# Six convolutions of v's first block between the last depthwise convolutions of q and k, on one Trainium2 core

## The chip, the cores and the metric

The kernel runs on one core of a Trainium2 chip. The metric is device time in microseconds (us) of one execution; lower is better. The engines go by the names of the profile: PE is TensorE (matrix products; PEld its weight loads), DVE is VectorE, ACT is ScalarE, POOL is GpSimd, SP is SyncE, which here only issues transfers (DMA). Each engine has its own list of instructions, and an instruction that waits for a semaphore holds what stands behind it in that list.

## The reference, cut to what matters

x has 384 channels and 192 x 192 pixels. Only layer 0 is touched by the change, and in it q, k and v up to the attention matrix:

```python
x = x + _L0_conv_ref(_gn(x), ...)
...
qkv = jnp.einsum('bchw,oc->bohw', x, w_qkv) + b_qkv[None, :, None, None]
qkv = qkv.reshape(b, 3 * c, hs, DS, ws, DS).max(axis=(3, 5))
qkv = lax.conv_general_dilated(qkv, w_dw, (1, 1), 'SAME', feature_group_count=3 * c, ...)
qkv = qkv + b_dw[None, :, None, None]
q, k, v = jnp.split(qkv, 3, axis=1)
...
attn = jnp.einsum('bhcn,bhdn->bhcd', q, k) * temperature[None]
out = _topk_softmax(attn, C // 2) @ v * a1 + _topk_softmax(attn, C * 2 // 3) @ v * a2 + ...
```

q and k are scaled to norm 1 over all pixels before `attn`, so attention needs all of q and k first. Each of q, k and v is a 1 x 1 convolution of the normalised x, a 2 x 2 maximum, and a 3 x 3 depthwise convolution. v is needed only after the top-k softmax. Layer 1, a 7 x 7 depthwise convolution of the sum, follows when all of layer 0 is done.

## The kernel before

The kernel has five stages: statistics of x (0 to about 100 us of the profiled execution), q and k (to about 1384 us), the attention matrix together with the first three blocks of v (to about 1491 us), the rest of v with the projection and the residual, and layer 1. The change lies at the border of the second and the third.

**q and k.** `for b in range(NB + 1)` (L688) runs over 24 blocks of 8 image rows. `pooled` (L592) makes, for each of the six channel groups of q and k (`ct`), three products of 512 columns in PSUM tiles `pq` (L604), and DVE takes their 2 x 2 maximum into a ring of rows (L612). One block behind, `depthwise` runs nine multiply-adds per group on DVE (`taps`, L645 and L647) into tiles `qk`, and `products` (L653) follows with the sums of squares on ACT (L656), the transposes on PE (L665), their copies to SBUF on ACT (L671), and the products of q and k, added up in the PSUM tile `grams` (L674). In the last pass, `b == NB`, there is no image block left: only the depthwise convolutions of block 23 and its `products` remain.

**Buffers.** x of q and k is loaded by SP into three buffers of `xpool`. The kernel divides PSUM into eight banks: one for `grams`, three for `ptr` (transposes and other small products), and four for `pq`. When q and k are done, `qx.close()` (L717) gives the four banks of `pq` to the pool `pv`, two tiles of two banks each, and `xctx.close()` gives the SBUF of `xpool` to what comes next: the row buffers `rows2` (filled at their borders by ACT, L508), the depthwise results `vb`, and six buffers `xp2` for x of v. A tile placed on memory that was in use before waits for the last users of that memory.

**v.** v is cut into 16 blocks (`order` sets their sequence; the first is block 13), each of six image strips `t0`, taken two at a time. `load_v` (L844) loads two strips with three transfers of 384 KB on SP (L848). `convolve` (L851) makes one of v's three channel groups for two strips: six matrix products of 384 columns (L858), which the trace shows as twelve records (1728 for 144 convolutions), and one DVE maximum of the result into rows (L864). With two `pv` tiles, a convolution can start only when the maximum of the one two before it is done.

**Attention.** `attention` (L722) is a Python generator. It takes the norms (`rn`, L725 to L728, with one step on POOL, L726), spreads them over the columns with three products against `dg_rk` (`along_free`, L218: L223 on DVE, L224 on PE, L225 on DVE), scales `grams` (L742), cuts the blocks of the heads out by small transfers (L750, issued by ACT and POOL), ranks each element against its row by fifteen DVE passes over 128 x 2304 elements (L767 to L775), makes the four softmaxes (L780 to L798), writes them into `diag` by small transfers (L804) and transposes that on PE into `attnT` (L811, L815). The loop over the first `AHEAD = 3` blocks of v draws this generator on by three steps after each pair of strips:

```python
        for i in range(AHEAD):
            for t0 in range(0, NT, UT):
                xb = load_v(i, t0)
                for ct in range(KT):
                    convolve(i, t0, ct, xb, lambda ins: ins)
                for _ in range(3):
                    next(chain, None)
```

**What sets the order.** Instructions outside a `keep` or `pin` are put in order on each engine by a scheduler at build time, by their dependencies and its own estimates of duration; so the order here is not that of the source. From block 4 of v on (`for i in range(AHEAD, NBC)`) the order on PE and DVE is written out by hand.

Of the kernel before, what the change touches and what calls it, by code (L numbers as in the profile page):

```python
# [8 lines left out]
F32 = mybir.dt.float32  # L9
AF = mybir.ActivationFunctionType  # L10
ALU = mybir.AluOpType
AX = mybir.AxisListType

P = 128
C = 384
KT = C // P
O3 = 3 * C
CT = O3 // P
HW = 192
PS = HW // 2  # L20
# [6 lines left out]
NB = PS // PR  # L27
# [24 lines left out]
TR = 32  # L52
# [17 lines left out]
RB = 2  # L70
NBC = TR // RB
PBC = NT * PS
UT = 2
FIRST = NBC - 3
# [4 lines left out]
def conv_preact_d2(  # L79
# [17 lines left out]
    nc = tc.nc  # L97
    PSUM = bass.MemoryType.PSUM
# [46 lines left out]
    wq = const.tile([P, KT, O3], F32, name="wq")  # L145
# [89 lines left out]
    def row_tiles(pool, name, n):  # L235

        t = pool.tile([P, n * KT * ROW], F32, name=name)
        rows = [
            t[:, k * ROW : (k + 1) * ROW].rearrange("p (t c) -> p t c", c=PS + 2)
            for k in range(n * KT)  # L240
        ]
        return [rows[k : k + KT] for k in range(0, n * KT, KT)], t

    vrows, rowbuf = row_tiles(rowp, "rows", 3)

    xctx = ExitStack()
    xpool = xctx.enter_context(tc.tile_pool(name="xpool", bufs=NX))
    parkp = xctx.enter_context(tc.tile_pool(name="parkp", bufs=1))

    def load_x(b, name):  # L250
        xb = xpool.tile([P, KT, BLK], F32, name=f"{name}{b}", tag="xb")
        nc.sync.dma_start(xb, xv[:, :, b * BLK : (b + 1) * BLK])
        return xb
# [5 lines left out]
    psx = ExitStack()  # L259
    pgram = psx.enter_context(tc.tile_pool(name="pgram", bufs=1, space=PSUM))  # L260
    gram = []
    for mt, (lo, hi) in enumerate(SPAN):
        o = sum(h - l for l, h in SPAN[:mt])
# [4 lines left out]
    qx = ExitStack()  # L268
# [21 lines left out]
    with tc.tile_pool(name="stp", bufs=1) as stp, tc.tile_pool(name="xsp", bufs=5) as xsp:  # L290
# [82 lines left out]
        for b in reversed(range(NB)):  # L373
            if b == NX - 1:
# [7 lines left out]
                for k, i in ((0, 0), (1, 1), (KT, 2)):  # L382
                    ps = total(f"gs_mid0_{k}", 1, terms[i])
# [6 lines left out]
            if b < NX:  # L390
                xb = held[b][:, 0:TWO]
            else:
                xb = xsp.tile([P, TWO, BLK], F32, name=f"xs{b}", tag="xs")
# [44 lines left out]
        kt = TWO  # L438
        mid = mids[:, kt : kt + 1]
        for b in [*range(NB - 2, NX, -2), NX, *reversed(range(NX))]:  # L440
            n = 2 if b > NX else 1
            if b == NX - 1:
                most = aggregate(kt, NX, NB, "most")
                ps = total(
                    "gs_mid0_2", 1,
                    [(sel(1, 2), means[1]), (shared[:, P:], me), (whole, most[:, 0:1])],
                )
# [5 lines left out]
            if b < NX:  # L453
                xb = held[b][:, kt]
            else:
                xb = xsp.tile([P, TWO, BLK], F32, name=f"xt{b}", tag="xs")
                xb = xb.rearrange("p k n -> p (k n)")[:, 0 : n * BLK]
# [3 lines left out]
        ps = total("gs0_2", 2, [(sel(1, 2), ds[1]), (shared[:, P:], de), (whole, d)])  # L461
# [23 lines left out]
    for i in range(3):  # L485
        w = wq[:, TWO, i * C : (i + 1) * C]
# [23 lines left out]
    def row_borders(tiles):  # L510
        for ct, t in enumerate(tiles):
            fill(t[:, :, 0 : PS + 2 : PS + 1], 2 * KT + ct, NT + 2, 2)
            fill(t[:, 0, :], 2 * KT + ct, PS + 2)
            fill(t[:, NT + 1, :], 2 * KT + ct, PS + 2)

    with ExitStack() as bx:
        padp = bx.enter_context(tc.tile_pool(name="padp", bufs=1))
        qkp = bx.enter_context(tc.tile_pool(name="qkp", bufs=9))
# [130 lines left out]
        def depthwise(b, ct, dst):  # L649
            r0 = b % 3 * PR  # L650
            taps(dst, ct, lambda i, j: ring[ct][:, r0 + i : r0 + i + PR, j : j + PS])

        def products(b, qk):  # L653
            for i in range(2 * KT):
                junk = trp.tile([P, PB], F32, name=f"junk{b}_{i}", tag="junk")
                nc.scalar.activation(  # L656
                    junk, qk[i].rearrange("p h w -> p (h w)"), AF.Square,
                    accum_out=ssq[:, i, b : b + 1],
                )
            for j in range(PB // P):  # L660
                sides = []
                for s in range(2):
                    ps = ptr.tile([P, C], F32, name=f"tr{b}_{j}_{s}", tag="tr")
                    for i in range(KT):
                        nc.tensor.transpose(  # L665
                            ps[:, i * P : (i + 1) * P],
                            qk[s * KT + i].rearrange("p h w -> p (h w)")[:, j * P : (j + 1) * P],
                            ident,
                        )
                    sb = trp.tile([P, C], F32, name=f"qkT{b}_{j}_{s}", tag=f"qkT{s}")  # L670
                    nc.scalar.copy(sb, ps)  # L671
                    sides.append(sb)
                for mt, (lo, hi) in enumerate(SPAN):
                    nc.tensor.matmul(  # L674
                        gram[mt],
                        sides[0][:, mt * P : (mt + 1) * P],
                        sides[1][:, lo:hi],
                        start=False,
                        stop=(b == NB - 1 and j == PB // P - 1),
                        skip_group_check=True,  # L680
                    )


        nc.tensor.matmul(
# [3 lines left out]
        for b in range(NB + 1):  # L688
            xb = None
            if b < NB:  # L690
                xb = held.pop(b) if b in held else load_x(b, "xq")
            qk = []
            for ct in range(2 * KT + 1):
                if b < NB and ct < 2 * KT:
                    if b == 0 and ct < 2:

                        if ct == 0:
                            pooled(b, 0, xb)
                            pooled(b, 1, xb)
                            biases()  # L700
                    else:
                        pooled(b, ct, xb)
                    bordered(b, ct)
                if b > 0 and ct > 0:
                    dst = qkp.tile([P, PR, PS], F32, name=f"qk{b}_{ct}", tag="qk")
                    qk.append(dst)
                    depthwise(b - 1, ct - 1, dst)
                    if ct == 2 * KT:
                        products(b - 1, qk)
            if b == 2:  # L710
                for tiles in vrows:
                    row_borders(tiles)
            if b < len(pieces):
                with tc.issue_after(stats0):
                    weights(*pieces[b])

    qx.close()  # L717
    xctx.close()

    near = {}  # L720
# [100 lines left out]
    rowp2 = dx.enter_context(tc.tile_pool(name="rowp2", bufs=1))  # L821
    vp = dx.enter_context(tc.tile_pool(name="vp", bufs=6))
    xp2 = dx.enter_context(tc.tile_pool(name="xp2", bufs=6))
    pv = psx.enter_context(tc.tile_pool(name="pv", bufs=2, space=PSUM))
    H = PBC // 2
    order = [(FIRST + i) % NBC for i in range(NBC)]

    vrows += row_tiles(rowp2, "rows2", 2)[0]
    for tiles in vrows[3:]:
        row_borders(tiles)  # L830

    def place(i):

        i %= NBC
        return vrows[i] if i < 2 else vrows[2 + (i - 2) % 3]

    def image_rows(ct, b, t0, nt):
        return bass.AP(
            x.tensor,
            x.offset + (ct * P * HW + t0 * TR + b * RB) * HW,  # L840
            [[HW * HW, P], [TR * HW, nt], [1, RB * HW]],
        )

    def load_v(i, t0):  # L844
        b = order[i]
        xb = xp2.tile([P, KT, UT, RB * HW], F32, name=f"xv{b}_{t0}", tag="xv")
        for kt in range(KT):
            nc.sync.dma_start(xb[:, kt], image_rows(kt, b, t0, UT))  # L848
        return xb

    def convolve(i, t0, ct, xb, pin):  # L851
        b, rows = order[i], place(i)
        o = (2 * KT + ct) * P
        ps = pv.tile([P, UT, 512], F32, name=f"pv{b}_{t0}_{ct}", tag="pv")
        for u in range(UT):
            for kt in range(KT):
                pin(
                    nc.tensor.matmul(  # L858
                        ps[:, u, 0 : RB * HW], wq[:, kt, o : o + P], xb[:, kt, u, :],
                        start=(kt == 0), stop=(kt == KT - 1),  # L860
                    )
                )
        pin(
            nc.vector.tensor_reduce(  # L864
                rows[ct][:, 1 + t0 : 1 + t0 + UT, 1 : PS + 1],
                ps[:, :, 0 : RB * HW].rearrange("p u (a w b) -> p u w a b", a=2, b=2),
                AX.XY,
                ALU.max,
            )
        )  # L870


    vbs, begun = {}, set()
# [29 lines left out]
    with tc.tile_pool(name="ap", bufs=1) as ap:  # L903
        chain = attention(ap)
        for i in range(AHEAD):
            for t0 in range(0, NT, UT):
                xb = load_v(i, t0)
                for ct in range(KT):
                    convolve(i, t0, ct, xb, lambda ins: ins)
                for _ in range(3):  # L910
                    next(chain, None)
            if i == AHEAD - 1:
                for ct in range(KT):
                    depthwise_v(1, ct, (0, 1))
        for _ in chain:
            pass
# [148 lines left out]
    for i in range(AHEAD, NBC):  # L1065
        j = i - 2
        xb = load_v(i, 0)
# [4 lines left out]
        xb = load_v(i, UT)  # L1072
# [9 lines left out]
        xb = load_v(i, 2 * UT)  # L1082
# [40 lines left out]
    with ExitStack() as ex_:  # L1123
# [97 lines left out]
        with tc.tile_pool(name="gps1", bufs=1, space=PSUM) as gps:  # L1221
            ps = over_groups(gps, mid1.unsqueeze(2), 1, "gs_mid1")
            gmid = const.tile([P, KT], F32, name="gmid")
            nc.vector.tensor_scalar_mul(gmid, ps[:, :, 0], 1.0 / GC)
            ps = over_groups(gps, about(mv1, gmid, "1"), 2, "gs1")
# [133 lines left out]
        last = None  # L1359
        for n in range(steps):  # L1360
# [9 lines left out]
            for q in range(CP):  # L1370
                ps = pc.tile([P, 2, 512], F32, name=f"pc{n}_{q}", tag="pc")
                for k in range(2):
                    i = 2 * q + k
# [9 lines left out]
                            start=False, stop=False,  # L1383
# [5 lines left out]
                            start=False, stop=True,  # L1389
# [20 lines left out]
            last = apart  # L1410
# [57 lines left out]
```

## Time and profile before

| what | value |
|---|---|
| median of 4 runs | 2834.36 us (2829.42 to 2846.21) |
| the profiled execution | 2846.21 us, its span 2844.5 us |
| granted PE clock over the span | 0.982 |
| PE busy | 2649.5 us, 93% of the span |
| DVE busy | 2319.8 us, 82% |
| ACT busy, POOL busy | 871.1 us (31%), 760.3 us (27%) |
| PE busy from 1240 to 1300 us (q and k, steady) | 59.95 of 60.00 us |
| PE busy from 1384.05 to 1399.17 us | 14.14 of 15.12 us |
| PE busy from 1399.17 to 1490.77 us | 91.60 of 91.60 us |
| DVE busy from 1399.17 to 1490.77 us | 78.62 of 91.60 us |
| PE busy from 1490.77 to 2844.5 us | 1287.82 of 1353.73 us |

The profiled execution is the slowest of the four runs, 11.85 us over their median; sums below are made within it. The span is the time from the first to the last instruction; 1.7 us of the execution lie outside it. Times of single instructions are counted in us from the start of the span. Busy shares are averages over stages with different limits: at the border of q, k and v PE is the busy engine on both sides, and a stretch of some 25 us between them is not full. A PE that is busy is not always at full speed: the column PEclk gives the clock that was granted, 1.00 being full.

### The profile page before, as it was taken

To read this page: it belongs to the slowest core of one execution; us is meant where nothing else is said; L and a number is where in the kernel's file an instruction comes from. 1 tells how busy PE (TensorE), PEld (TensorE's weight loads), DVE (VectorE), ACT (ScalarE), POOL (GpSimd) and SP (SyncE) were. 2 spreads that over 40 slices of the span, in tenths; PEclk is the share of its full clock that TensorE was granted. 3 is DMA by queue.
4 is the path that set the end of the run, shared out by engine and by line. 5 is a ranking of instruction groups with operands and counts; after the bars stand their busy time and mean duration, and the time that the engine had idled before them with its cause. 6 is when DMAs were issued, how large, how long until landed. Compare 5 with 4: busy or idle time off the path is not lost.

```text
span 2844.5 us, 25466 instructions
## 1 busy us (share of the span) xinstructions
PE 2649.5 (93%) x8671; PEld 1585.0 (56%) x8671; DVE 2319.8 (82%) x3382; ACT 871.1 (31%) x1637; POOL 760.3 (27%) x884
## 2 busy tenths in 40 slices
PE   0399999999999999999899989999998699999997
PEld 0244444444444454444556656666666477777776
DVE  7989887878878788788688878888889678777776
ACT  0141111111111111111102322222324467777775
POOL 1034444000000000000102330010101467788887
PEclk9999999999999999999999999999999799999999
DMA  9966766201011010100336998575666899999997
GB/s 382 401 237 223 250 202 232 100 34 67 34 53 47 34 67 33 39 28 0 134 103 211 335 363 270 176 250 187 227 222 216 295 313 356 372 366 372 366 371 249
DMA packets 236401, 584.52 MB, mean 205 GB/s; under 512 B 16704, under 2 KB 168112, under 8 KB 219504
## 3 DMA queue, kind: packets, MB, share of 16 engines
q1 hardware_dynamic: 175344, 286.77, 29.2%
q0 software_dynamic: 37376, 148.85, 15.4%
q10 hardware_dynamic: 23552, 147.27, 13.8%
q8 instruction: 69, 1.13, 0.2%
q14 instruction: 60, 0.49, 0.0%
HBM read 374.47 MB, written 208.21 MB: 205 GB/s over the span
## 4 chain that ended last, share of the span: by engine, by line
PE 79%; DMA 12%; DVE 5%; POOL 2%; ACT 1%; issue 1%; SPq 0%; ACTq 0%; POOLq 0%; DVEq 0%
PE pq L604 37%; PE pv L858 19%; DMA out_dram<-res 6%; PE pr L970 4%; PE pc L1387 3%; PE pc L1376 3%; PE pc L1381 3%; PE po L946 3%; DMA xs<-in_x_dram 2%; PE grams L674 2%; PE tr L665 2%; PE pq_begun L423 1%; DVE st L318 1%; DVE vb L892 1%; DMA xv<-in_x_dram 1%; DMA sd<-sx 1%
## 5 line engine op out<-in xcount | busy, mean ns | idle before, releaser
L604 PE MATMUL pq<-xq,wq 128*128 128x512 f32 x2268 | 990.7, 592 | 0.0
L604 PEld LDWEIGHTS pq<-xq,wq 128*128 128x128 f32 x2268 | 423.0, 190 | 492.2 <-issue 447.0
L647 DVE SCALAR_TENSOR_TENSOR qk<-ring,wd,qk 128x384 f32<-128x384 f32 x1152 | 674.1, 612 | 20.9 <-ACT ring L634 7.1
L858 PE MATMUL pv<-xv,wq 128*128 128x384 f32 x1728 | 567.4, 489 | 10.2 <-DMA xv<-in_x_dram 9.2
L858 PEld LDWEIGHTS pv<-xv,wq 128*128 128x128 f32 x1728 | 329.5, 191 | 237.1 <-DMA xv<-in_x_dram 8.0
L612 DVE TENSOR_REDUCE ring<-pq 128x128 f32<-128x512 f32 x428 | 293.7, 687 | 190.7 <-PE pq L604 189.9
L1400 DVE TENSOR_SCALAR apart<-pc,rb 32x576 f32<-32x576 f32 x384 | 312.3, 813 | 128.8 <-PE pc L1387 111.5
L1398 ACT ACTIVATE apart<-pc,rb 32x576 f32<-32x576 f32 x384 | 281.4, 733 | 146.5 <-PE pc L1387 141.7
L892 DVE SCALAR_TENSOR_TENSOR vb<-rows,wd,vb 128x576 f32<-128x576 f32 x384 | 313.0, 817 | 11.2
L1387 PE MATMUL pc<-aux,h 128*128 128x288 f32 x768 | 251.0, 408 | 4.2 <-POOL aux L1309 2.7
L1376 PE MATMUL pc<-main,w 128*128 128x288 f32 x768 | 251.7, 409 | 0.3 <-issue 0.3
L1381 PE MATMUL pc<-main,w 128*128 128x288 f32 x768 | 250.9, 408 | 0.0
L1004 DVE TENSOR_TENSOR sx<-xr,y 128x576 f32<-128x576 f32 x192 | 217.5, 1174 | 39.1 <-ACT y L978 23.4
L656 ACT ACTIVATE junk<-qk 128x384 f32<-128x384 f32 x144 | 75.4, 523 | 541.7 <-DVE qk L647 541.7
L1346 POOL COPY res<-apart 128x1152 f32<-128x1152 f32 x96 | 212.7, 2247 | 90.6 <-DMA out_dram<-res 63.8
L755 POOL MEMSET lower<- 128x2304 f32 x1 | 2.0, 2018 | 871.7 <-PE grams L674 871.7
L1045 POOL DMA_DIRECT2D sd<-sx x96 | 72.2, 756 | 511.3 <-DVE sx L1004 491.8
L864 DVE TENSOR_REDUCE rows<-pv 128x192 f32<-128x768 f32 x144 | 137.5, 956 | 67.8 <-PE pv L858 67.6
L1387 PEld LDWEIGHTS pc<-aux,h 128*128 128x128 f32 x768 | 145.6, 190 | 48.6 <-POOL aux L1324 4.2
L1381 PEld LDWEIGHTS pc<-main,w 128*128 128x128 f32 x768 | 146.6, 191 | 42.0
L1376 PEld LDWEIGHTS pc<-main,w 128*128 128x128 f32 x768 | 146.2, 191 | 42.4 <-issue 1.0
L1024 ACT ACTIVATE wq<-sx,negmid 128x1152 f32<-128x1152 f32 x96 | 120.6, 1257 | 101.3 <-DVE sx L1004 97.2
(214 smaller groups left out, 2348.3 us busy)
## 6 DMA issues: line engine op xcount, KB each, us to landing
sd<-sx POOLq DMA_DIRECT2D x96, 600.0 KB, 10.3
xv<-in_x_dram SPq DMA_DIRECT2D x144, 384.0 KB, 5.1
xr<-in_x_dram SPq DMA_DIRECT2D x48, 1152.0 KB, 15.1
out_dram<-res SPq DMA_DIRECT2D x192, 288.0 KB, 10.8
main<-sd ACTq DMA_DIRECT2D x46, 1200.0 KB, 9.9
xq<-in_x_dram SPq DMA_DIRECT2D x21, 2304.0 KB, 8.8
w<-wt ACTq DMA_DIRECT2D x46, 1024.0 KB, 7.0
xs<-in_x_dram SPq DMA_DIRECT2D x24, 1536.0 KB, 15.1
```

The lines of the kernel that those rows point to most:

```text
L604: nc.tensor.matmul(ps, wq[:, kt, ct * P : (ct + 1) * P], rows[:, kt, :, g * 64 : (g + 1) * 64], start=(kt == 0), stop=(kt == KT - 1), skip ...
L612: nc.vector.tensor_reduce(t[:, r0 : r0 + PR, 1 + g * 32 : 1 + (g + 1) * 32], ps.rearrange("p (h a w b) -> p h w a b", h=PR, a=2, b=2), AX. ...
L647: nc.vector.scalar_tensor_tensor(dst, src, w, dst, ALU.mult, ALU.add)
L858: nc.tensor.matmul(ps[:, u, 0 : RB * HW], wq[:, kt, o : o + P], xb[:, kt, u, :], start=(kt == 0), stop=(kt == KT - 1),)
L892: pin(nc.vector.scalar_tensor_tensor(dst, src, w, dst, ALU.mult, ALU.add))
L1004: nc.vector.tensor_tensor(bass.AP(flat.tensor, flat.offset + at(e) + a * RUN, [flat.ap[0], [JP, NT], [1, NJ], [at(f) - at(e), 2]],), xq[:, ...
L1346: keep(nc.gpsimd.tensor_copy(res[:, k], apart[:, :, k].rearrange("p e n -> p n e")))
L1376: nc.tensor.matmul(acc, w[:, i, 0:P], main[:, i, :, 0:NJ], start=True, stop=False)
L1381: nc.tensor.matmul(acc, w[:, i, P : 2 * P], main[:, i, :, 1 : 1 + NJ], start=False, stop=False,)
L1387: nc.tensor.matmul(acc, h[:, i], aux[:, i, :, 0:NJ], start=False, stop=True,)
L1398: keep(nc.scalar.mul(dst, src, scale))
L1400: keep(nc.vector.tensor_scalar_mul(dst, src, scale))
```

## The change

The three helpers `order`, `place` and `image_rows`, and `convolve`, are moved up unchanged, ahead of the stage on q and k. In the last pass of that stage (`b == NB`) the banks of `pq` are now released at its start and `pv` opened there; x of the first four strips of v's first block is loaded into a buffer of `xpool` (three transfers of 768 KB on SP); and after every second depthwise convolution (`ct` 2, 4 and 6) two of the six convolutions on these strips are put into the program. `products` returns its last matrix product, and in the loop over the first three blocks of v the remaining 21 convolutions are to be issued only after it. The third pair of strips of the first block still uses `load_v`. Nothing is computed that was not computed before, and nothing is left out.

```diff
             xb = None
             if b < NB:
                 xb = held.pop(b) if b in held else load_x(b, "xq")
+            else:
+
+                qx.close()
+                pv = psx.enter_context(tc.tile_pool(name="pv", bufs=2, space=PSUM))
+                xb = xpool.tile([P, KT, 2 * UT, RB * HW], F32, name="xv_begun", tag="xb")
+                for kt in range(KT):
+                    nc.sync.dma_start(xb[:, kt], image_rows(kt, order[0], 0, 2 * UT))
             qk = []
...
                     depthwise(b - 1, ct - 1, dst)
+                    if b == NB and ct % 2 == 0:
+                        for n in range(ct - 2, ct):
+                            t0 = n // KT * UT
+                            convolve(0, t0, n % KT, xb[:, :, t0 : t0 + UT], lambda ins: ins)
                     if ct == 2 * KT:
-                        products(b - 1, qk)
+                        multiplied = products(b - 1, qk)
...
-    qx.close()
     xctx.close()
...
         for i in range(AHEAD):
             for t0 in range(0, NT, UT):
-                xb = load_v(i, t0)
-                for ct in range(KT):
-                    convolve(i, t0, ct, xb, lambda ins: ins)
+                if i > 0 or t0 == 2 * UT:
+                    xb = load_v(i, t0)
+                    with tc.issue_after(multiplied):
+                        for ct in range(KT):
+                            convolve(i, t0, ct, xb, lambda ins: ins)
                 for _ in range(3):
                     next(chain, None)
```

In `products` the loop's last statement keeps the instruction for the caller:

```diff
-                    nc.tensor.matmul(
+                    last = nc.tensor.matmul(
...
-                    )
+                    ).ins
+            return last
```

## The prediction

> **What bounds the kernel now.** The chain of waits first: PE holds 79% of it.
>
> ```profile
> PE 79%; DMA 12%; DVE 5%; POOL 2%; ACT 1%; issue 1%; SPq 0%; ACTq 0%; POOLq 0%; DVEq 0%
> ```
>
> The chain by time shows where PE is not its holder near the change: DVE (`qk` L647) from 1359.58 to 1376.91 us, then POOL and DVE (`lower`, `rn`, `dg_rk`) from 1384.1 to 1392.1. The timeline of PE there (start, duration, instructions, in brackets the idle time before and its releaser):
>
> ```profile
> 1359.38 1.56 PE L665 MATMUL tr<-ident,qk 128*128 128x128 f32 x10
> ...
> 1370.37 1.33 PE L665 MATMUL tr<-ident,qk 128*128 128x128 f32 x5 [2.74 <-DVE qk L647]
> ...
> 1376.93 0.69 PE L665 MATMUL tr<-ident,qk 128*128 128x128 f32 x2 [3.55 <-DVE qk L647]
> 1378.00 3.57 PE L674 MATMUL grams<-qkT,qkT 128*128 128x144 f32 x12 [0.38 <-ACT qkT L671]
> ```
>
> PE waits for the last depthwise convolutions, and works slowly in between: the same twelve products took 1.79 us at 1312.80. The table of windows has the clock (columns: PE, PEld, DVE, ACT, POOL busy, PEclk, DMA share, GB/s):
>
> ```profile
> 1367.00:1369.00 2.00, 0.63 (x5) 0.42 (x3) 2.00 (x5) 1.87 (x8) 0.00 (x0) 1.00 0.00 0
> 1369.00:1371.00 2.00, 0.63 (x3) 0.63 (x4) 2.00 (x5) 0.62 (x2) 0.00 (x0) 0.55 0.00 0
> 1371.00:1373.00 2.00, 1.64 (x9) 1.23 (x7) 1.93 (x5) 0.99 (x3) 0.00 (x0) 0.50 0.00 0
> ...
> 1383.00:1385.00 2.00, 2.00 (x11) 1.55 (x11) 0.30 (x1) 0.00 (x0) 0.84 (x1) 1.00 1.04 375
> ```
>
> From 1399 us PE is full again; the timeline of DVE shows what runs beside it, and that the attention matrix is early:
>
> ```profile
> 1399.01 91.75 PE L858 MATMUL pv<-xv,wq 128*128 128x384 f32 x284
> 1490.60 0.93 PE L811 MATMUL aT<-ident,diag 128*128 128x128 f32 x7
> ```
> ```profile
> 1384.24 0.30 DVE L725 TENSOR_REDUCE rn<-ssq 128x6 f32<-128x144 f32 x1 [7.36 <-PE grams L674]
> ...
> 1388.81 2.40 DVE L223 TENSOR_SCALAR dg_rk<-ident,rn 128x128 f32<-128x128 f32 x2
> ...
> 1472.54 0.30 DVE L798 TENSOR_TENSOR mix<-mix,em 128x144 f32<-128x144 f32 x1
> 1475.32 0.96 DVE L864 TENSOR_REDUCE rows<-pv 128x192 f32<-128x768 f32 x1 [2.49 <-PE pv L858]
> ```
>
> `mix` is done at 1472.84; its transfers are issued until 1476 and land 1.6 to 1.8 us later, some 13 us before PE comes to `aT`.
>
> **What the skill says.** The Trainium skill, "TensorE: Matmul & The Clock Gate", Part 1, says that an idle window of about 3.4 us halves PE's clock and about 3.4 us of work restore it. The trace agrees roughly: 1.00 before 1369, 0.50 from 1371, back some 5 us after work resumed at 1378.0. "SBUF — State Buffer", section "Who interferes with whom", says that DVE's fast two-port forms and POOL exclude each other for a whole instruction; here one of the three `dg_rk` took 2.209 us against a median of 0.285, and ended with POOL's `affine_select` (1388.48 to 1390.93).
>
> **The most that can be had.** From 1359.38 to `aT` at 1490.60 are 131.2 us. PE's own work in them: 27 convolutions of twelve records at 0.3226 us (284 records in 91.6 us), 3.87 us each, 104.5 us; two blocks' `tr` and `grams` at 4.7 us (8.12 us from 1308.34 to 1316.46, less eight `pq` records, 3.4 us), 9.4; `tps` and `af_rk`, 1.7. Sum 115.6. Idle time and half clock are thus 15.6 us, 0.55% of the execution: the ceiling. On every engine the lists before this stretch and from block 4 of v on hold the same instructions in the same order in both programs (only SP has three transfers fewer, in the stretch), so a gain at `aT` shifts what follows by as much.
>
> **Part by part.** I lay durations of the trace along the changed program's lists.
>
> *The six convolutions*: 72 records, 23.2 us of PE, all ahead of block 23's transposes. The load of 3 x 768 KB waits only for block 21's products (done by about 1257 us) while DMA is idle: hidden. The banks of `pq` are free when DVE's last maximum ends (1360.28): no wait. Block 22's transposes and products are interleaved with the first convolution and end at about 1368.0 (8.6 us of PE from 1359.4); the other five follow without a stop, to 1387.4. DVE has 16.5 us of `qk` and four maxima of 0.95 us inside it; each falls due in time (about 1368.7, 1373.8, 1377.9, 1380.8), because DVE's 0.53 to 0.63 us per multiply-add leaves a gap for every 3.87 us of PE.
>
> *Products later*: in the new list all transposes of block 23 stand behind the sixth convolution; they need `qk`, ready at 1380. From 1387.4: transposes, ACT's copies (0.42 us each, with two and then seven border fills of 0.26 us ahead of or among them; these fills now wait for the sixth convolution, since `rows2` lies on its x), products; PE idles about 1 us in bits. Last product at about 1393.1, against 1384.05: 9.0 us later.
>
> *The load of the third pair*: it and all of v's loads behind it on SP now wait for the sixth convolution, 1387.4 instead of 1377.0, for memory. A load lands 3.4 to 8.4 us after issue, median 4.7: about 1392.2, just before PE can use it at 1393.1. I take 0; at worst about 2 us. Later loads are needed 3.87 x 3 us apart and are not late.
>
> *The norms*: the chain from the last product to `dg_rk` is the old one, with `lower` (2.02 us, POOL) ahead of `rn` again: 7 us, to 1400.1. In the old list PE had 17 products of v ahead of it (34 records); in the new one only five (ten records, 3.2 us), then `af_rk` waits. PE stands from 1396.3 to 1400.1: 3.8 us. Half clock afterwards: the 2.74 us gap at 1367.6 was followed by it, so I count it, 2.3 us for PE; below 0 it cannot cost.
>
> So at about 1402.6 PE has done 84 records where the old run had done about 51: a lead of 33 records, 10.7 us.
>
> *The attention chain on DVE* starts 9 us late with fewer convolutions left beside it (19 maxima instead of 23 at its first pass). The new DVE list puts three passes of 2.55 us (`rank`, `eq`, `gt` of the second and third third) between two maxima, and later two maxima side by side. Laid out: `gt` begins at 1408.8; maxima at 1413.7, 1417.2, 1420.6, 1424.1, 1430.1, 1433.5, 1437.0; then the three passes to 1445.4, while PE has finished block 14's eighth convolution at 1442.7 and needs the seventh's tile, free at 1446.35: PE waits 3.6 us. After that DVE stays a little ahead; `mix` ends at 1477.1, its transfers at 1481.8, PE's last convolution at 1485.1. At full clock after the norms the same sum gives 1483.9. So `aT` starts at about 1484.6, 6.0 us early.
>
> Sum within the profiled execution: 15.6 ceiling, less stops that replace the old: 1.0 (copies), 3.8 (`af_rk`), 0 to 2.3 (clock, partly swallowed by the next), 3.6 (PSUM tile behind DVE), about 1 for waits on semaphores: 5 to 7. 2846.21 - 6 = 2840.2. The median of the shown runs is 11.85 us lower; I take the gain as the same: 2834.36 - 6 = 2828.4.
>
> **Rivals.** (1) *PE stays the bound after the norms*: the load is on time, and DVE's order doesn't stall PE. For it: DVE was busy only 78.62 of 91.60 us in that stretch. Against: the order of the list is fixed, and three passes in a row leave PE without a tile. It gives the lead of 10.7 to 11.5 us: 2823. (2) *Slower: the attention chain becomes the path.* Place: from the last product to `aT`. In the old run the chain takes 1384.05 to 1477.5, 93.5 us, and has 13 us to spare; it now starts 9.0 us late, so from 97.5 us on the kernel is slower. By my sum it shortens to 88.7, mostly as four maxima of 0.95 us are gone from it; if late loads (the burst of 27 filled DMA from 1379 to 1399 in the old run), the small `att` transfers behind that burst, and PE at half clock hold DVE's maxima, which stand between its passes, it grows. Price: 3 us above break-even at 100 us: 2837. (3) *Returned later*: a fixed transfer rate in the rest of v takes the gain back, 0: 2834. For: DMA share 0.84 after 1490.77. Against: those transfers are issued by the same shifted lists.
>
> **Chances.** Forecast 0.62, rival 1 0.16, rival 2 0.14, rival 3 0.08. A measurement of this kernel tells about 0.5%, 14 us, from no change. The ceiling of 15.6 us hardly passes that, rival 2 would need a chain of 112 us; with the spread of the runs (2829 to 2846) faster by over 0.5% gets 0.11, slower 0.05, same 0.84. The range holds the cases and the spread of a median: 2819 to 2839.
>
> **What would show it.** PE: six convolutions between 1360 and 1388 with no gap over 1 us; the last `grams` near 1393; a gap of about 4 us before `af_rk`; a gap of 3 to 4 us released by DVE `rows` near 1443; `aT` near 1484.6; and the same distance from `aT` to the end. It is wrong if `aT` lies outside 1479 to 1490, or if that distance changes.

## The result, and the profile after

| | before | after |
|---|---|---|
| median | 2834.99 us (64 runs) | 2830.55 us (43 runs) |
| ratio to before | | 0.9983, 95% interval 0.9974 to 0.9991 |
| profiled execution, its span | 2846.21, 2844.5 us | 2836.47, 2834.8 us |

The changed kernel takes 4.4 us less; the interval makes it 2.6 to 7.4 us. Predicted were 6.0. A second set of runs agrees: 22 of the changed kernel with a median of 2831.61 us against 33 of before with 2837.43 us, ratio 0.9981 (0.9969 to 0.9992).

The spans differ by 9.7 us, and not all of it is the change. I measure from here on D, the distance from the first `tr` behind the last `pq` to the first `aT` on PE: in before from 1359.38 to 1490.60, 131.2 us. In after PE's timeline has (start, duration, line and engine, operation, records, in brackets the idle time ahead and its releaser):

```profile
1355.54 1.50 PE L700 MATMUL tr<-ident,qk 128*128 128x128 f32 x10
...
1364.32 19.51 PE L537 MATMUL pv<-xv_begun,wq 128*128 128x384 f32 x60
1383.67 1.67 PE L700 MATMUL tr<-ident,qk 128*128 128x128 f32 x12
...
1389.33 3.39 PE L537 MATMUL pv<-xv,wq 128*128 128x384 f32 x10
1396.61 1.20 PE L224 MATMUL af_rk<-dg_rk,ones 128*128 128x128 f32 x4 [3.89 <-DVE dg_rk L223]
...
1441.68 38.97 PE L537 MATMUL pv<-xv,wq 128*128 128x384 f32 x120 [3.05 <-DVE rows L543]
1480.49 0.93 PE L857 MATMUL aT<-ident,diag 128*128 128x128 f32 x7
```

D is 124.95 us, 6.3 less. The stage begins 3.8 us earlier in this execution, which came from the stages ahead of it, where both programs hold the same instructions in the same order but for the three early transfers. PE's clock from 190 to 200 us was 0.83 in before and 1.00 in after; it was 0.83 in both_orders too (an experiment below), whose program is after's up to this stretch and which begins it at 1358.69. So I take the 3.8 us as spread between executions; no run isolates them. From `aT` to the end it is 1353.9 us before and 1354.3 after. So 3.8 + 6.3 - 0.4 is the difference of the spans. D is what the change moved.

The table of windows shows the two halves of D and the rest (columns: PE, PEld, DVE, ACT, POOL busy, PEclk, DMA share, GB/s):

```profile
1355.54:1389.43 33.89, 33.87 (x152) 23.14 (x151) 22.41 (x37) 12.10 (x40) 0.00 (x0) 1.00 0.12 41
1389.43:1480.49 91.06, 84.08 (x260) 49.13 (x259) 80.32 (x92) 1.51 (x6) 11.87 (x14) 0.98 0.43 142
1480.49:2834.80 1354.31, 1287.96 (x4786) 910.29 (x4784) 1100.39 (x1268) 652.54 (x1009) 584.87 (x596) 0.97 0.84 290
```

To the last product PE is full and at full clock: the three stops for DVE `qk` are gone. Of the next 91 us it stands 7.0, in two stops: 3.89 us for `dg_rk` and 3.05 us for a maximum. What holds the second is in the timeline of DVE: three ranking passes in a row, then two maxima that PE has been waiting for.

```profile
1433.29 2.54 DVE L821 TENSOR_REDUCE rank<-gt 128x48 f32<-128x2304 f32 x1
1435.75 2.54 DVE L815 TENSOR_TENSOR eq<-att 128x2304 f32<-128x2304 f32 x1
1438.21 2.54 DVE L813 TENSOR_TENSOR gt<-att 128x2304 f32<-128x2304 f32 x1
1440.68 1.81 DVE L543 TENSOR_REDUCE rows<-pv 128x192 f32<-128x768 f32 x2
```

The chain of waits over the whole span has changed little, as most of the span is the other stages:

```profile
PE 79%; DMA 11%; DVE 6%; ACT 1%; POOL 1%; issue 1%; ACTq 0%; SPq 0%; POOLq 0%; DVEq 0%
```

### The profile page after: what moved, and what is told of

It reads as the page before. It is cut to its first block, busy times and chain, and to the rows that moved or that the text cites. A ratio compares the mean times of both kernels' runs of the same rounds, so it can differ in the third digit from the quotient of the medians.

```text
span 2834.8 us, 25467 instructions
## 1 busy us (share of the span) xinstructions
PE 2644.3 (93%) x8671; PEld 1581.1 (56%) x8671; DVE 2314.4 (82%) x3382; ACT 871.1 (31%) x1637; POOL 762.8 (27%) x884
## 4 chain that ended last, share of the span: by engine, by line
PE 79%; DMA 11%; DVE 6%; ACT 1%; POOL 1%; issue 1%; ACTq 0%; SPq 0%; POOLq 0%; DVEq 0%
PE pq L639 37%; PE pv L537 18%; DMA out_dram<-res 6%; PE pr L983 4%; PE pc L1400 4%; PE pc L1389 3%; PE pc L1394 3%; PE po L959 3%; DMA xs<-in_x_dram 2%; PE grams L709 2%; PE tr L700 2%; PE pq_begun L423 1%; DVE st L318 1%; DVE vb L903 1%; DMA aux<-sh 1%; DMA sd<-sx 1%
## 5 line engine op out<-in xcount | busy, mean ns | idle before, releaser
L537 PE MATMUL pv<-xv,wq 128*128 128x384 f32 x1656 | 545.4, 490 | 11.4 <-DVE rows L543 6.6
L537 PEld LDWEIGHTS pv<-xv,wq 128*128 128x128 f32 x1656 | 316.2, 192 | 229.8 <-DVE rows L543 8.9
## 6 DMA issues: line engine op xcount, KB each, us to landing
sd<-sx POOLq DMA_DIRECT2D x96, 600.0 KB, 10.5
```

Of the source, the lines that this page charges most:

```text
L537: nc.tensor.matmul(ps[:, u, 0 : RB * HW], wq[:, kt, o : o + P], xb[:, kt, u, :], start=(kt == 0), stop=(kt == KT - 1),)
```

## The experiments

All of them are read by D, because single executions of one kernel spread over more than 20 us (after: 2822.41 to 2844.28).

| kernel | D, us | PE's stops over 0.6 us behind the last `grams` |
|---|---|---|
| before, before_again | 131.2, 131.4 | `rows`, about 1.0 each (the stops for `qk` lie ahead of the last `grams`) |
| after, after_again, after_third | 125.0, 127.6, 127.4 | `dg_rk` 3.89 each; `rows` 3.05, 2.74, 2.74 |
| six_behind | 139.2 | `dg_rk` 0.80, `xv` 1.74, `rows` 3.76 |
| three_ahead | 129.2 | `dg_rk` 0.80, `xv` 1.81, `rows` 0.94 |
| af_late | 128.6 | `dg_rk` 0.70, `rows` 1.38, 5.52, 0.92 |
| chain_late | 134.7 | `dg_rk` 3.60, `rows` 2.74, `diag` 7.04 |
| dve_order | 121.7 | `dg_rk` 2.49, `rows` 0.79 |
| both_orders | 119.1 | none |
| orders_mended | 117.2 | `rows` 0.83 |

**Is it the filled gaps? six_behind.** The load, its buffer and the early banks stay; the convolutions go behind the products.

```diff
-                    if b == NB and ct % 2 == 0:
-                        for n in range(ct - 2, ct):
-                            t0 = n // KT * UT
-                            convolve(0, t0, n % KT, xb[:, :, t0 : t0 + UT], lambda ins: ins)
                     if ct == 2 * KT:
                         multiplied = products(b - 1, qk)
+                    if b == NB and ct == 2 * KT:
+                        with tc.issue_after(multiplied):
+                            for n in range(2 * KT):
+                                t0 = n // KT * UT
+                                convolve(0, t0, n % KT, xb[:, :, t0 : t0 + UT], lambda ins: ins)
```

> D (first `tr` after the last `pq` to the first `aT` on PE) is 131.2 us before, 125.0 us after. Here the early load, the buffer and the early banks stay as in after, and the six convolutions are issued only behind the last product of q and k. Theory (the gain is PE's filled gaps alone; the load from the buffer and the banks bring nothing): the stops for DVE `qk` and the half clock are back, about 25 us to the last `grams` as in before; moreover the load of the third pair waits for the sixth convolution, so PE stops some 4 us there: D is 133 to 137, worse than before. Rival (the early load and the early banks carry the gain): D stays near 125.

D was 139.2. PE's timeline:

```profile
1366.42 1.33 PE L700 MATMUL tr<-ident,qk 128*128 128x128 f32 x5 [2.85 <-DVE qk L682]
...
1372.97 0.69 PE L700 MATMUL tr<-ident,qk 128*128 128x128 f32 x2 [3.48 <-DVE qk L682]
1374.05 3.57 PE L709 MATMUL grams<-qkT,qkT 128*128 128x144 f32 x12 [0.38 <-ACT qkT L706]
...
1407.57 7.98 PE L537 MATMUL pv<-xv,wq 128*128 128x384 f32 x24 [1.74 <-DMA xv<-in_x_dram]
1419.30 75.49 PE L537 MATMUL pv<-xv,wq 128*128 128x384 f32 x228 [3.76 <-DVE rows L543]
```

The old stops for `qk` are back, and the twelve products take 3.57 us again; the last product ends after 24.8 us, in before after 24.7. So the early load and banks carry nothing by themselves; the rival is out. The load of the third pair is issued at 1404.17, behind the sixth convolution, and PE waits for it, 1.74 us where I had expected some 4: the buffer has a price, which after pays under the products of block 23. The 3.76 us for a maximum I had not expected; DVE's timeline has the reason:

```profile
1413.35 2.56 DVE L814 TENSOR_TENSOR gt<-att 128x2304 f32<-128x2304 f32 x1 [5.93 <-DMA att<-scaled]
1415.83 2.55 DVE L816 TENSOR_TENSOR eq<-att 128x2304 f32<-128x2304 f32 x1
1418.30 0.95 DVE L543 TENSOR_REDUCE rows<-pv 128x192 f32<-128x768 f32 x1
```

The small transfers into `att` now run at the same time as the late loads. They land 5.1 us after issue in the median, in after 2.8, and DVE waits 5.93 us for them, with two passes and then PE's maximum behind them in its list. (In after the wait is 0.59 us, but there other work fills part of the 3.1 us between `scaled` and `gt`.) It is the place that the prediction's second rival named, in a kernel where the loads come late. With the half clock behind it (0.96 and 0.61 in the two windows of 4 us from 1416), it puts D 2 us above the theory's range.

**How many? three_ahead.** After every second depthwise convolution one convolution instead of two, the other three behind the products.

```diff
-                        for n in range(ct - 2, ct):
-                            t0 = n // KT * UT
-                            convolve(0, t0, n % KT, xb[:, :, t0 : t0 + UT], lambda ins: ins)
+                        n = ct // 2 - 1
+                        convolve(0, 0, n, xb[:, :, 0:UT], lambda ins: ins)
...
+                            for n in range(KT):
+                                convolve(0, UT, n, xb[:, :, UT : 2 * UT], lambda ins: ins)
```

> D is 131.2 us before, 125.0 us after. Here three of the six convolutions stay ahead of block 23's products and three stand behind them. Theory (every convolution placed in the gaps is worth its 3.87 us until about 10.6 us of gaps are full, but the load of the third pair, which waits for the sixth, is now late by about 4 us): last `grams` 26 to 28 us after the start (before 24.7, after 33.9), a stop of about 4 us for the load before the first convolution of the third pair, no stop of 3.9 us before `af_rk`, D 126 to 129. Rival (three would do, because the norms and the ranking then start 6 us earlier): D 124 or less.

The last product ended at 27.7 us, as expected. Then:

```profile
1394.83 0.61 PE L224 MATMUL af_rk<-dg_rk,ones 128*128 128x128 f32 x4
1396.24 0.49 PE L224 MATMUL af_rk<-dg_rk,ones 128*128 128x128 f32 x2 [0.80 <-DVE dg_rk L223]
1398.54 10.95 PE L537 MATMUL pv<-xv,wq 128*128 128x384 f32 x24 [1.81 <-DMA xv<-in_x_dram]
1410.43 73.80 PE L537 MATMUL pv<-xv,wq 128*128 128x384 f32 x228 [0.94 <-DVE rows L543]
```

Between the end of the sixth convolution (1395.0) and the first on the third pair PE has 3.5 us with only 1.1 us of work, and 24 records behind it take 10.95 us instead of 7.9: half clock. The stop for the load is 1.81 us, not the 4 expected. D was 129.2, 0.2 above the range. The clock was low twice, the first time behind stops of at most 1.45 us:

```profile
1376.00:1380.00 4.00, 3.86 (x19) 3.51 (x19) 0.00 (x0) 1.43 (x4) 0.00 (x0) 0.66 0.00 0
1380.00:1384.00 4.00, 4.00 (x13) 3.38 (x13) 0.30 (x1) 0.00 (x0) 1.29 (x1) 0.50 0.00 0
```

Each time costs up to some 3.4 us of PE's work (4 x (0.34 + 0.50) here, and 4 x (0.28 + 0.50 + 0.07) in the three windows from 1396 to 1408), 6.8 in all; after lost 1.7 to 5.1 us in this way, as the part on the firmness of D works out. So this one execution does not show that three ahead are worse than six: the clock alone can make the difference of 1.6 to 4.2 us. The rival, D of 124 or less, did not come true. Three ahead with the third pair loaded earlier was not tried.

**Which of after's two stops costs? af_late.** The matrix products of the norms stand behind 18 products of v instead of 5; DVE's order is left to the scheduler.

```diff
-        along_free(rkb, rn[:, KT : 2 * KT], ptr, "rk", "tr")
+        with tc.issue_after(done[0]):
+            along_free(rkb, rn[:, KT : 2 * KT], ptr, "rk", "tr")
...
-                for _ in range(3):
+                for _ in range(3 if i > 0 else 9 if t0 == 2 * UT else 0):
                     next(chain, None)
```

(`done[0]` is the last product of v traced by then.)

> D is the distance from the first `tr` after the last `pq` to the first `aT` on PE: 131.2 us before, 125.0 us after. Here `af_rk` stands behind 18 products of v (36 records) instead of 5 (10 records); the order on DVE follows by itself and now has four ranking passes in a row (`rank`, `eq`, `gt`, `eq`) between two maxima, and three of them once more. Theory (what the change leaves is two stops of PE, and the second is set by the order on DVE): the stop of 3.9 us before `af_rk` and the half clock behind it go, but PE then stops for DVE `rows` about 5 to 6 us and once more 3 to 4 us, so D is 126 to 128: no gain. Rival (the stop before `af_rk` is the whole loss and DVE keeps up): D falls by about 4 to 5 us, to 120 to 121.

The stop of 3.89 us is gone and D is 128.6, no better than after:

```profile
1415.83 11.88 PE L539 MATMUL pv<-xv,wq 128*128 128x384 f32 x36 [1.38 <-DVE rows L546]
1433.23 10.67 PE L539 MATMUL pv<-xv,wq 128*128 128x384 f32 x24 [5.52 <-DVE rows L546]
1444.82 38.97 PE L539 MATMUL pv<-xv,wq 128*128 128x384 f32 x120 [0.92 <-DVE rows L546]
```

All of it comes back as stops for DVE, which now has four passes between two maxima, as its timeline shows:

```profile
1422.36 2.54 DVE L825 TENSOR_REDUCE rank<-gt 128x48 f32<-128x2304 f32 x1
1424.82 2.55 DVE L819 TENSOR_TENSOR eq<-att 128x2304 f32<-128x2304 f32 x1
1427.28 2.55 DVE L817 TENSOR_TENSOR gt<-att 128x2304 f32<-128x2304 f32 x1
1429.75 2.55 DVE L821 TENSOR_TENSOR eq<-eq,lower 128x2304 f32<-128x2304 f32 x1
1432.22 0.95 DVE L546 TENSOR_REDUCE rows<-pv 128x192 f32<-128x768 f32 x1
```

The rival (the stop before `af_rk` is the whole loss and DVE keeps up) is out. As DVE's order changed along with PE's, this run does not weigh the two stops against each other; the next two do.

**DVE's order: dve_order, both_orders.** The 21 convolutions, their maxima and the steps of `attention` are traced in a written order, held by `keep` on PE and DVE. One word stands for one convolution, traced first; then `M` is the maximum of the oldest open one, `c` the next step of `attention` (with one ranking pass each), `t` a multiply-add of `vb`.

```diff
+        plan = 'ccc Mcctt Mtcc Mc Mc Mc Mc Mcc Mc Mc Mc Mc Mcc Mc Mccc Mcc Mc M Mttttt Mttttt MtttttM'.split()
+        late = []
+        for n, acts in enumerate(plan):
...
+                convolve(i, t0, ct, xb, keep, late)
+            for act in acts:
+                if act == "M":
+                    late.pop(0)()
...
+                elif act == "c":
+                    next(chain)
```

In both_orders the same is done with the norms further back, so that `af_rk` stands behind three convolutions, and with three tiles `dg_rk` instead of two. In both, `tps` has moved behind the last products, and a stop of 0.68 us for ACT opens ahead of these.

```diff
-        plan = 'ccc Mcctt Mtcc Mc Mc Mc Mc Mcc Mc Mc Mc Mc Mcc Mc Mccc Mcc Mc M Mttttt Mttttt MtttttM'.split()
+        plan = 'c Mc Mc Mcctt Mtcc Mc Mc Mc Mc Mcc Mc Mc Mc Mc Mcc Mc Mccc Mcc Mcttttt Mttttt MtttttM'.split()
```

> D is 131.2 us before and 125.0 us after. Here PE's order is that of after but for one product ahead of `af_rk`, and DVE's order is written out: one ranking pass, twice two, between two maxima of v. Theory: the stop before `af_rk` stays (3 to 4 us, with its short half clock), the stop of 3.05 us for DVE `rows` goes and no other takes its place, so D is 120 to 122. Rival (DVE's total work in the stretch, not its order, holds PE): the stop only moves to a later maximum and D stays at 124 to 125.

> D is 131.2 us before and 125.0 us after; PE's own work in it is about 115.6. Here `af_rk` stands behind three whole convolutions and DVE's order is written out as in dve_order. Theory (the two stops are all that the change leaves): no stop of PE over 0.6 us between the last `grams` and `aT`, the clock stays at 1.00, `mix` is done about 9 us before PE comes to `aT`, D is 117 to 118.5, and the time some 13 us under before and 7 us under after, as the distance from `aT` to the end (1354 us) stays. Rival (the attention chain becomes the path once PE has no stops): PE stops before `aT`, D 120 to 125. Rival (what is gained at `aT` is given back later): D 117 to 118.5 but the distance from `aT` to the end grows to 1360.

dve_order: D 121.7. The stop before `af_rk` is 2.49 us; that for DVE has shrunk to 0.79, and up to `aT` no other over 0.3 takes its place. The clock stayed at 1.00, where I had expected a short half clock, so a part of the distance to after (125.0 to 127.6) is the clock:

```profile
1395.83 0.68 PE L793 MATMUL af_rk<-dg_rk,ones 128*128 128x128 f32 x4 [2.49 <-DVE dg_rk L792]
...
1409.56 46.71 PE L538 MATMUL pv<-xv,wq 128*128 128x384 f32 x144 [0.79 <-DVE rows L544]
```

both_orders: D 119.1, 0.6 above the range, with no stop over 0.6 us behind the last `grams` and the clock at 1.00 throughout; its median was 2826.96 us against 2837.43 of before, ratio 0.9964 (0.9949 to 0.998). Both stops are thus mainly DVE's and PE's order: DVE does the same ranking passes and softmaxes in all of them. Its work up to `aT` is not quite the same, 102.7 us in after, 100.1 in dve_order and 96.4 in both_orders, as some multiply-adds of `vb` now stand behind `aT`. There PE stops for DVE `rows`, for 0.87 us in dve_order and for 1.56 and 0.87 us in both_orders, and not at all in after; so a part of the gain in D is paid back there.

**The small rest: orders_mended.** both_orders still stops four times for 0.23 to 0.51 us, and twice behind `aT`. Here nine of the eighteen `t`, instead of three, stand ahead of the first ranking pass, where DVE waits for the norms and for `att`; their own order is changed too. The doubled passes are spread, and `tps` stands ahead of the last product, as in after.

```diff
-        plan = 'c Mc Mc Mcctt Mtcc Mc Mc Mc Mc Mcc Mc Mc Mc Mc Mcc Mc Mccc Mcc Mcttttt Mttttt MtttttM'.split()
+        plan = 'c Mtttc Mtttc Mccttt Mc Mc Mcc Mc Mc Mc Mc Mcc Mc Mc Mc Mcc Mcc Mcc Mccttt Mttt MtttM'.split()
```

> D is 131.2 us before, 125.0 and 127.6 us in two runs of after, 119.1 us in both_orders, where PE still stops four times for DVE `rows` for 0.2 to 0.5 us (each with about 0.27 us for the first product behind it), 0.7 us before the last products, and twice more (1.6 and 0.9 us) just behind `aT`. Here nine multiply-adds of `vb` are moved from the end of the stretch into DVE's early idle time, the two ranking passes in a row are spread evenly, and `tps` stands ahead of the last products again. Theory (these small stops come from DVE being late by what was packed into its last slots): D 117 to 118, the stop behind `aT` at most 0.9 us, the time 1 to 4 us under both_orders, about 13 us under before. Rival (DVE is simply full here): D stays at 119.

```profile
1386.81 11.77 PE L538 MATMUL pv<-xv,wq 128*128 128x384 f32 x36
1398.42 0.83 PE L795 MATMUL af_rk<-dg_rk,ones 128*128 128x128 f32 x6
1399.09 66.33 PE L538 MATMUL pv<-xv,wq 128*128 128x384 f32 x204
1466.25 4.14 PE L538 MATMUL pv<-xv,wq 128*128 128x384 f32 x12 [0.83 <-DVE rows L544]
1470.22 0.93 PE L871 MATMUL aT<-ident,diag 128*128 128x128 f32 x7
```

One stop is left, and D is 117.2, 1.6 above PE's own work of 115.6. No stop follows behind `aT`, and DVE's work up to there is 100.3 us. The median of 9 runs is 2821.66 us, against 2835.12 of before in 14 runs: 0.9951 (0.9932 to 0.9969). By this ratio the version beats both kernels (after had 0.9983, 0.9974 to 0.9991); the two were not measured side by side.

**How far is the attention chain from the path? chain_late.**

```diff
+        for _ in range(14):
+            nc.scalar.copy(ex, mix)
+            nc.scalar.copy(mix, ex)
         diag = ap.tile([P, KT, C], F32, name="diag")
```

> D is 131.2 us before, 125.0 us after. Here 28 copies of `mix` on ACT, about 8 us in a row, are put between the last `mix` and the transfers into `diag`; nothing else moves and no result changes. It asks how far the attention chain is from the path. Theory (in after the chain's last transfer lands some 3.7 us before `aT`): PE stops before `aT` for the added time less 3.7 us, about 4 us, D about 129. Rival (the chain is as far from the path as in before, 13 us): no stop, D 125. Rival (it is already on it): D 133.

The copies took 0.34 us each, from 1473.71 to 1483.35, so 9.6 us instead of 8. PE's and ACT's timelines:

```profile
1489.57 1.95 PE L860 MATMUL aT<-ident,diag 128*128 128x128 f32 x7 [7.04 <-DMA diag<-mix]
```
```profile
1483.35 3.30 ACTq L853 DMA_DIRECT2D diag<-mix  x5
```

9.6 us of delay make a stop of 7.0, so the chain had 2.6 us to spare, in place of the 3.7 I had expected. The other two theories, 13 us to spare and none, are out. The 2.6 us are a low figure, because the delayed transfers fell into other transfers (DMA share 0.98 and 1.06 from 1484 to 1488) and took longer to land. From issue to landing they took 4.8 to 5.5 us here, 2.6 to 3.5 in after and 1.6 to 1.8 in before. As an estimate from this, in after itself the last of them, issued at 1474.3, has landed by 1477.8, which leaves 2.7 us or somewhat more before `aT` at 1480.49. In before the last is issued at 1475.4, which leaves the 13 us of the prediction.

**How firm is D? after_again, before_again, after_third.** No edit.

> The changed kernel once more, for the spread of D from run to run. Theory: D within 0.7 us of 124.95, the distance from `aT` to the end within 2 us of 1354.3, while the start of the stretch moves by some us with the statistics stage; the total ratio to before is near 0.998. Rival (the 6.3 us at `aT` were themselves such a spread): D differs by 3 us or more.

> The kernel before once more, for the spread of D, which was 125.0 and 127.6 us in two runs of after: PE's clock falls to half behind some of its stops of 2.7 to 3.9 us and not behind others. Theory: before has only one such place (the stops for DVE `qk`, where PE waits for DVE in any case), so D is within 1 us of 131.2 and PE's clock is 1.00 from the last `grams` to `aT`. Rival (D of before spreads as that of after): 129 or less, or 133 or more.

> The changed kernel a third time. Theory: D is between 124.5 and 128, and what it has above 124.5 stands as half clock behind the stop before `af_rk` and behind the stop for DVE `rows`: half clock behind both gives about 127.5, behind the first alone about 125. Rival (the spread has another source): D outside of this, or not accounted for by the clock within 0.7 us.

before gave 131.4, within 0.2 of the first, and its clock was 1.00 from the last `grams` to `aT` as expected. after gave 127.6 and 127.4, neither within 0.7 of the first nor 3 off: here my theory for after_again failed. The table of windows shows why. First after, then after_again:

```profile
1396.00:1400.00 4.00, 3.40 (x10) 2.59 (x11) 1.81 (x5) 0.00 (x0) 0.38 (x1) 0.57 0.92 312
1400.00:1404.00 4.00, 4.00 (x14) 2.37 (x13) 3.96 (x9) 0.00 (x0) 2.40 (x5) 1.00 0.37 112
...
1444.00:1448.00 4.00, 4.00 (x14) 2.36 (x13) 4.00 (x4) 0.00 (x0) 0.00 (x0) 1.00 0.28 46
```
```profile
1396.00:1400.00 4.00, 3.16 (x9) 2.46 (x10) 1.81 (x4) 0.00 (x0) 0.61 (x1) 0.51 0.94 315
1400.00:1404.00 4.00, 4.00 (x9) 2.21 (x8) 3.68 (x8) 0.00 (x0) 2.17 (x5) 0.63 0.42 129
...
1444.00:1448.00 4.00, 4.00 (x9) 2.22 (x8) 4.00 (x3) 0.00 (x0) 0.00 (x0) 0.59 0.00 0
```

In after the clock is low in one of these windows, which loses 4 x 0.43 = 1.7 us; in after_again in three, which loses 4 x (0.49 + 0.37 + 0.41) = 5.1 us. The difference of 3.4, less 0.3 by which the second stop is shorter, is 3.1; D differs by 2.6. after_third has half clock behind both stops too (0.50 and 0.79, then 0.83 and 0.75), and D of 127.4, as expected for that case. The median gain of 4.4 us lies between the three values of 131.3 - D (131.3 is the mean of the two of before): 6.3, 3.8 and 3.9.

**Is the gain given back behind `aT`?** From `aT` to the end the profiled executions range from 1335 to 1354 us, those of one kernel too (before 1353.9 and 1340.9), so single runs can't tell. In six_behind, three_ahead and chain_late, run together, D is 139.2, 129.2 and 134.7, and the rest is 1336.5, 1336.2 and 1335.2: there it doesn't follow D. In before_again, after_third and orders_mended, also run together, it is 1340.9, 1351.4 and 1353.4, longer where D is shorter. The medians decide: orders_mended gains 14.1 us in D and 13.5 in the median (8.8 to 19.3 by the interval), both_orders 12.2 and 10.5 (5.7 to 14.5). So the gain is not given back as a whole; that a few us of it are, these intervals can't exclude.

## Why the prediction was right, and where its sizes were off

The forecast, the likeliest case, held by place and by sign. By its steps, times from the stage's start in before (1359.38) and after (1355.54):

- *Six convolutions without a stop*, their end predicted at 28.0 us: 28.1. PE was busy 33.87 of 33.89 us to the last products.
- *Last product 9.0 us later*, at 33.7: 33.9.
- *The third pair's load costs 0*: no stop there. That it was a cover and not a gift is shown by six_behind and three_ahead, where PE waits for it.
- *PE stands 3.8 us before `af_rk`*: 3.89, three times.
- *PE waits 3.6 us for a PSUM tile behind DVE's passes*: 3.05, 2.74, 2.74.
- *Half clock after the norms, 2.3 us*: the mis-sized term. It was 1.7 us in the first run and 3.4 in after_again; and behind the second stop the prediction counted none, where after_again has 1.6. The forecast of 6.0 was thus good for the profiled execution (6.3), which had the best clock of the three, and that much is luck; it was too high for the other two (3.8, 3.9), and against the median it is 1.6 us too much.
- *The closing sum*: 15.6 less 1.0, 3.8, 3.6, about 1 and 0 to 2.3 is 3.9 to 6.2, not the "5 to 7" that stands there; the 6.0 comes from the times laid out before it. In after what is lost of the 15.6 is 9.3: 3.89 and 3.05 for the stops, 1.7 for the clock, nothing for ACT's copies, and some 0.7 for the rest.
- *`aT` at 125.2 us*: 125.0, 127.6, 127.4.
- *Rival 1 (PE stays the bound after the norms)* failed for the reason given: DVE's fixed order. dve_order shows that the stop goes with the order. *Rival 2 (the chain becomes the path)* did not happen, and was near: the sum left 3.3 us between the last transfer and PE, chain_late shows 2.6. *Rival 3 (the gain is returned later)* fell with the medians above, as far as it says all of the gain.

Of the ceiling of 15.6 us the change takes 4 to 6, because two stops and their half clock replace the old ones; orders_mended takes 14.1.

## What to carry to other kernels

A gap on the busy engine that is filled with later work moves everything that hung on the order of that later work: look what else used to stand between the same waits (here the cover of the norms and the maxima between ranking passes), and give it a new cover in the same edit. Where two engines hand tiles to and fro with two buffers, look at the longest run of other work between two releases and not only at the sum of work: one 2.5 us pass between two maxima of 0.9 us held PE's 3.87 us step, three did not. When the difference is a fifth of a per cent, measure a distance inside the profile, over several executions, and compare the clock granted in it.

## What the runs showed of the hardware that I had not expected

Whether half clock follows a stop of PE of about 3 us differs from one execution to the next. The stop of 3.89 us was followed by it each time, which cost 1.7 us of PE's work in after and 3.4 in after_again; one of 2.74 us was followed by it in after_again, after_third and chain_late; one of 3.05 us in after was not, nor was one of 2.49 us in dve_order. The Trainium skill, "TensorE: Matmul & The Clock Gate", Part 1, says that the window by which activity is judged runs freely, so that the place of the change depends on where work falls in it; the runs agree in that the same program has it in one execution and not in another. They don't agree with its 3.4 us as the least idle time: 2.74 us sufficed, and in three_ahead the clock fell behind three stops of 0.16, 1.45 and 0.64 us with transposes between them (PE busy 1.87 of 4.00 us from 1372 to 1376).

DVE's `dg_rk` shows what its neighbour costs: in both_orders three of them took 0.67 us together, when POOL's `affine_select` had ended (1397.07 to 1399.52, `dg_rk` at 1401.24); in after two took 2.32 us beside it.
